# Four-layer graph network: edge sums begun by a flag instead of a zero product, and denominators cut at column 320

## The chip, the core and the metric

The kernel runs on one core of a Trainium2 chip. A core has a matrix engine (TensorE, in profiles PE, its weight loads PEld), a vector engine (VectorE, DVE), an activation engine (ScalarE, ACT), a general engine (GpSimd, POOL) and an engine that here only issues transfers (SyncE, SP). Products land in PSUM[...]. The metric is the time of the whole program on the device, in microseconds; lower is better.

## What is computed

There are 2708 nodes with 256 features, `x`, and one dense 2708 x 2708 matrix `adj` that is mostly zero. Four layers follow each other, each as `x = layernorm(x + layer(x))`. Layers 1 and 2, cut to what matters here:

```python
# layer 1: attention with 4 heads of 64 columns, all over the same mask
h = (x @ W).reshape(n, heads, head_dim)
e = src[:, :, None] + dst.T[None, :, :]
e = jnp.where(e > 0, e, ALPHA * e)
e = jnp.where(adj[:, None, :] > 0, e, NEG_INF)
out = jnp.einsum('nhm,mhd->nhd', jax.nn.softmax(e, axis=-1), h)
# layer 2, its first sum: the "edge sums"
node_support = node_adj_norm @ h        # adj without its diagonal, times x
edge_output = _gru_cell(node_support, h, edge_Wih, edge_Whh, edge_bih, edge_bhh)
```

The softmax of layer 1 needs for every node and head a sum of weighted features (the numerator, 64 values) and a sum of the weights alone (the denominator). Layer 2 then goes on with three attention heads over the same matrix, a second gated cell and layer 3's product.

## The kernel before, in words

The nodes are cut into 22 tiles of 128, the last with 20 rows. `adj` comes transposed, so that a block has source nodes on partitions and destination nodes along its columns. All products are float32; each float32 product leaves two records of a matmul in the profile.

**Layer 1.** Destinations are taken in six spans of tiles (4, 4, 4, 4, 3, 3), two at a time, so there are three groups: 1024, 1024 and 660 columns, the last made of spans of 384 and 276. For each group the heads are taken in two pairs (`q` = 0, 1), and for each pair the 22 source tiles `c` in turn. For each `c` VectorE makes two weight tiles `p`, one per head (L835). `heads` (L814, its product L817) multiplies 64 features of each head with `p` and sums into `acc[s]`, one bank for each span `s`, with the two heads in the two halves of the partitions. `totals` (its product L826) does the same with 32 columns of `h`, whose last is the one that gives the denominator; the four products of one `c`, two spans by two heads, go to the four 32-partition quarters of one bank, `den`. Quarter `j = 2 * (s ^ q) + i` belongs to span `s` and head `i`. The order is totals, heads for even `c` and heads, totals for odd `c`, so blocks of 16 records of one kind follow each other. At the end of a pair ScalarE copies both `acc` (L848) and then the two halves of `den` (L852) to SBUF. `step` weaves in the rows of the group before, in small steps: `layer1_end` (L683) transposes sums and denominators, divides, adds and normalises twice, with steps on ScalarE, VectorE (L679, L705, L708, L727, L730) and GpSimd (L680); `layer1_logits` (L748) transposes the finished rows on TensorE (L756) and multiplies them (L773). After the last group that group's own `layer1_end` runs beside the first edge sums.

**Layer 2's edge sums.** `raw_sums` (L354) works on six ranges `r` of 226 columns (the last 224) in each half of the destinations. For each of 11 pairs of source tiles it loads a block `pa` on SP's queue (five buffers), clears the diagonal on GpSimd (L286), and calls `seven` (L309), which forms three sums and a difference on VectorE (L315 to L318) and multiplies seven times (L328): a block product of two by two with seven products instead of eight. The seven results live in four banks: `m1` alone, and `m26`, `m75`, `m43` with two of them each, side by side. A product with `start=True` begins a sum; one without adds to what is there. Since two sums share a bank, before each range a product of a tile of zeros with a zero column (L359) is written over the whole of each shared bank with `start=True`, and the products in the shared banks carry no start flag (`not (one_bank and i)`). At the end of a range `gathered` (L332) reads the banks: ScalarE copies `m1` (L336), and VectorE adds the others to it in four steps (L339, L342, L345, L346). The result goes through a gated cell (L1062) for the first four ranges, with the sums one range ahead of the cells.

The order of instructions on each engine is drawn up by a scheduler from the program; the engines execute in that order and wait for each other by semaphores. Pools give out buffers in turn, and a new tile waits for the last reader of its buffer.

Of the kernel before, what the change touches and what calls it, by code (L numbers as in the profile page):

```python
# [10 lines left out]
BF16 = mybir.dt.bfloat16  # L11
# [8 lines left out]
P = 128  # L20
# [7 lines left out]
def kernel(  # L28
# [24 lines left out]
    nc = tc.nc  # L53
# [8 lines left out]
    W = GT * P  # L62
    CT = 32
# [28 lines left out]
    def width(lo, hi):  # L92
        return min(hi * P, N) - lo * P
# [19 lines left out]
    const = ctx.enter_context(tc.tile_pool(name="const", bufs=1))  # L113
# [5 lines left out]
    make_identity(nc, ident)  # L119
    offdiag = const.tile([P, P], F32, name="offdiag")  # L120
    nc.vector.tensor_scalar(offdiag, ident, -1.0, 1.0, ALU.mult, ALU.add)
    zeros = const.tile([P, P], BF16, name="zeros")
    nc.gpsimd.memset(zeros, 0.0)
    neg_half = const.tile([P, 1], F32, name="neg_half")
    nc.gpsimd.memset(neg_half, -0.5)

# [182 lines left out]
    def seven(pool, m, pa, b, tt, c, w, start, stop, slots, one_bank=False):  # L309

        m1, m26, m75, m43 = m
        a11, a21, a12, a22 = [pa[:, j, i, :w] for j in range(2) for i in range(2)]
        s = pool.tile([P, 3, pa.shape[3]], F32, tag="s", name="s", bufs=2)
        s1, s2, s4 = (s[:, i, :w] for i in range(3))
        nc.vector.tensor_tensor(s1, a21, a22, ALU.add)  # L315
        nc.vector.tensor_tensor(a21, a21, a11, ALU.subtract)  # L316
        nc.vector.tensor_tensor(s2, s1, a11, ALU.subtract)
        nc.vector.tensor_tensor(s4, a12, s2, ALU.subtract)  # L318
        for i, (dst, lt, rt) in enumerate((
            (m1, b[2 * c][:, :P], a11),  # L320
            (m26[:, 0], b[2 * c + 1][:, :P], a12),
            (m75[:, 0], tt[:, 2], a21),
            (m75[:, 1], tt[:, 0], s1),
            (m26[:, 1], tt[:, 1], s2),
            (m43[:, 0], tt[:, 3], a22),
            (m43[:, 1], b[2 * c + 1][:, P:], s4),
        )):
            nc.tensor.matmul(dst[:, :w], lt, rt, start=start and not (one_bank and i), stop=stop and not (one_bank and i in (1, 2, 5)))  # L328
            if i in slots:
                between()  # L330

# [22 lines left out]
    def raw_sums(pool, ps, keep, r):  # L354

        a, w = raws[r]
        m = [ps.tile([P, 2, W // 2], F32, tag=nm, name=nm) for nm in ("m1", "m26", "m75", "m43")]
        for b in m[1:]:
            nc.tensor.matmul(  # L359
                b.rearrange("p i w -> p (i w)"), zeros, zeros[:, :1].to_broadcast([P, W]), start=True, stop=False  # L360
            )
        m[0] = m[0][:, 0]
        for c in range(MH):
            pa = pool.tile([P, 2, 2, w], F32, tag="pa", name="pa", bufs=5)
            load_pairs(raws, r, c, pa)
            clear_own(raws, r, c, pa)
            if r == 0:
                xq.append(quarter_sums(keep, xs, c, "xq"))
            seven(pool, m, pa, xs, xq[c], c, w, c == 0, c == MH - 1, (), True)
            if c == MH - 1:  # L370
                y, _ = gathered(pool, m, w, w, "supt", 2)
                y = y.rearrange("p f h w -> p f (h w)")
                if r in left:
                    nc.scalar.dma_start(sup_d[r], y)
                edges.append(y)
            yield
# [27 lines left out]
    if True:  # L404
# [12 lines left out]
        if True:  # L417
# [38 lines left out]
            with pool("l0", 2) as l0:  # L456
# [48 lines left out]
                with pool("prep", side="right") as prep:  # L505
# [100 lines left out]
                    s = load_strip(l0, t)  # L606
# [21 lines left out]
                for t in range(ahead + 2, NT - 1):  # L628
                    s = load_strip(l0, t)
# [8 lines left out]
                s = load_strip(l0, t)  # L638
# [22 lines left out]
            if True:  # L661
# [123 lines left out]
                dens = [keepr.tile([P, W], F32, name=f"den{s}") for s in range(2)]  # L785
                for g in range(0, len(spans), 2):
                    segs = spans[g : g + 2]
                    at, w = segs[0][0] * P, width(segs[0][0], segs[-1][1])
                    if g >= 4:
                        falls.append(fallp.tile([P, H, 2 * W], F32, tag="fall_b", name="fall_b"))  # L790
                        for i in range(len(segs)):
                            load_fall(falls[-1], g + i, nc.sync)
                    cols = [(lo * P - at, width(lo, hi)) for lo, hi in segs]
                    sums, steps, halves = [], [itertools.chain(*rest)] if g == 0 else [], []

                    def step(c):
                        for s in list(steps):
                            if next(s, s) is s:
                                steps.remove(s)

                        if q == 0 and c % 5 == 1 and len(halves) < len(ended):
                            halves.append(layer1_end(l1, ended[len(halves)]))
                            next(halves[-1])
                            steps.append(itertools.islice(halves[-1], 2))

                        if q == 1 and c % 5 == 0 and c // 5 < len(halves):
                            steps.append(itertools.chain(halves[c // 5], [None], layer1_logits(ended[c // 5])))
                            next(steps[-1])

                    for q in range(H // 2):  # L810
                        den = ps_acc.tile([P, W], F32, tag="acc", name="den")
                        acc = [ps_acc.tile([P, W], F32, tag="acc", name="acc") for _ in segs]

                        def heads(c, ps, flags):  # L814
                            for s, (p0, ws) in enumerate(cols):
                                for i in (1, 0):
                                    nc.tensor.matmul(  # L817
                                        acc[s][i * HD : (i + 1) * HD, :ws], hs[c][:, 2 * q + i, :HD],
                                        ps[i][:, p0 : p0 + ws], **flags,
                                    )  # L820

                        def totals(c, ps, flags):
                            for s, (p0, ws) in enumerate(cols):
                                for i in (1, 0):
                                    j = (2 * (s ^ q) + i) * CT
                                    nc.tensor.matmul(  # L826
                                        den[j : j + CT, :ws], hs[c][:, 2 * q + i, HD + 1 - CT :],
                                        ps[i][:, p0 : p0 + ws], **flags,
                                    )

                        for c in range(NT):
                            ps = []
                            for i in range(2):
                                p = l1.tile([P, 2 * W], F32, tag="p", name="p", bufs=5)
                                nc.vector.scalar_tensor_tensor(  # L835
                                    p[:, :w], falls[g // 2][:, 2 * q + i, :w], rise[:, c, 2 * q + i : 2 * q + i + 1],
                                    mask[:, c, at : at + w], ALU.max, ALU.mult,
                                )
                                ps.append(p)

                            for part in (heads, totals)[:: -1 if c % 2 == 0 else 1]:
                                part(c, ps, dict(start=(c == 0), stop=(c == NT - 1)))
                                if part is (totals, heads)[c % 2]:
                                    step(c)
                        got = []
                        for s, (p0, ws) in enumerate(cols):
                            sb = keepr.tile([P, W], F32, tag=f"sum{q}{s}", name=f"sum{q}{s}")
                            nc.scalar.copy(sb[:, :ws], acc[s][:, :ws])  # L848
                            got.append(sb)
                        for s, (p0, ws) in enumerate(cols):  # L850
                            two = slice(2 * (s ^ q) * CT, 2 * ((s ^ q) + 1) * CT)
                            nc.scalar.copy(dens[s][two, :ws], den[two, :ws])  # L852
                        sums.append(got)
                    for a in steps:
                        for _ in a:
                            pass
                    ended = [(t, s, sums, dens, t - segs[0][0]) for s, (lo, hi) in enumerate(segs) for t in range(lo, hi)]
                    ended = [ended[i : i + 2] for i in range(0, len(ended), 2)]
# [24 lines left out]
                for i in range(SPLITS):  # L883
                    part = u_parts[:, :, i * K : (i + 1) * K]
# [7 lines left out]
                for t in range(NT):  # L892
                    for b, acc in zip(banks, pus):
                        w = width(*spans[b[0]])
                        for j, g in enumerate(b):
# [3 lines left out]
                                start=(t == 0), stop=(t == NT - 1),  # L899
# [801 lines left out]
```

## Time and profile before

| | us |
|---|---|
| median of 3 runs | 1865.03 (1864.9 to 1866.25) |
| the profiled execution | 1865.35 |
| its span, first to last instruction | 1863.6 |
| TensorE busy in it | 1832.7 |
| VectorE busy in it | 1280.9 |
| ScalarE busy in it | 699.3 |

The profile is of one execution. Its span leaves out what lies before the first and after the last instruction. A group's line gives engine, operation, output and inputs, shapes, how many there were, busy time, mean duration of one in ns, and the idle time of the engine before them with what ended it. A timeline's line gives start, length, engine and instructions that follow each other, with the idle time before. Ends of matmuls are modelled and hold their drain, so the distance from one start to the next is what a product costs in a stream; a few matmul records are missing.

### The profile page before, as it was taken

The numbers are of one execution on the slowest core, as the hardware profiler recorded it, in microseconds if no ns is written. First come the engines' busy times: TensorE is split into PE (matmuls) and PEld (weight loads), VectorE is DVE, ScalarE is ACT, GpSimd is POOL, SyncE is SP. The second block draws the span as 40 slices with busy tenths as digits, with TensorE's granted clock in tenths as the row PEclk, the third lists the DMA queues.
The fourth block names the chain that finished last, engine by engine and source line by source line (L and its number), as shares of the span: only waits on it lengthen the run. The fifth ranks groups of instructions, "written<-read, shape, count | busy, mean of one in ns | idle before, by whom it ended". The sixth has DMA issues, their size and how long they took to land. (4 is left out here: it accounts for less than half of the span.)

```text
span 1863.6 us, 23088 instructions
## 1 busy us (share of the span) xinstructions
PE 1832.7 (98%) x7526; PEld 1035.4 (56%) x7530; DVE 1280.9 (69%) x2263; ACT 699.3 (38%) x1442; POOL 266.4 (14%) x427
## 2 busy tenths in 40 slices
PE   9999999999999999999999999999999999999997
PEld 7788832233345887887444444444445556654555
DVE  5344489999897664754568888776887768844664
ACT  3544410033144203111546655555665556321011
POOL 1211220001012411000002000111200302111111
PEclk9999999999999999999999999999999999999999
DMA  8344410100002667754647666454554545634764
GB/s 298 133 148 151 168 30 1 30 1 12 12 7 71 144 144 186 182 130 114 182 131 207 176 174 171 123 159 114 165 151 121 135 106 141 167 106 116 203 163 121
DMA packets 435101, 237.32 MB, mean 127 GB/s; under 512 B 184363, under 2 KB 422348, under 8 KB 432540
## 3 DMA queue, kind: packets, MB, share of 16 engines
q1 hardware_dynamic: 422414, 208.66, 41.4%
q0 software_dynamic: 8208, 22.59, 3.9%
q10 hardware_dynamic: 4350, 4.50, 0.7%
q8 instruction: 62, 1.02, 0.2%
q14 instruction: 67, 0.55, 0.1%
HBM read 223.00 MB, written 12.66 MB: 126 GB/s over the span
## 5 line engine op out<-in xcount | busy, mean ns | idle before, releaser
L835 DVE SCALAR_TENSOR_TENSOR p<-fall_b,rise,mask 128x1024 f32<-128x1024 f32 (+1 forms) x264 | 293.9, 1156 | 32.5 <-PE den L826 16.7
L1328 ACT ACTIVATE p<-st,e_neg 128x1024 f32<-128x1024 f32 (+1 forms) x198 | 197.3, 1040 | 193.9 <-PE m L328 190.1
L328 PE MATMUL m<-s,xq 128*128 128x512 f32 (+3 forms) x660 | 230.1, 467 | 0.0
L817 PE MATMUL acc<-p,h 128*64 128x512 f32 (+2 forms) x1056 | 214.5, 548 | 0.2 <-ACT sum L848 0.2
L328 PE MATMUL m<-p,xq 128*128 128x512 f32 (+1 forms) x396 | 183.0, 544 | 0.1
L215 PE MATMUL acc<-turn,strip 128*128 128x257 f32 x792 | 181.8, 379 | 0.0
L1331 ACT ACTIVATE p<-p 128x1024 f32<-128x1024 f32 (+1 forms) x198 | 178.8, 942 | 0.2
L315 DVE TENSOR_TENSOR s<-p 128x512 f32<-128x512 f32 (+3 forms) x132 | 81.5, 618 | 136.6 <-PE m L328 112.7
L328 PE MATMUL m<-p,x 128*128 128x512 f32 (+1 forms) x396 | 167.7, 542 | 0.3 <-DVE supt L345 0.3
L328 PEld LDWEIGHTS m<-s,xq 128*128 128x128 f32 x660 | 124.5, 190 | 76.3 <-issue 59.2
L1332 DVE TENSOR_TENSOR p<-p,blk 128x1024 f32<-128x1024 f32 (+1 forms) x132 | 142.8, 1101 | 33.6 <-ACT p L1331 23.1
L215 PEld LDWEIGHTS acc<-turn,strip 128*128 128x128 f32 x792 | 147.2, 190 | 20.3
L817 PEld LDWEIGHTS acc<-p,h 128*64 128x64 f32 x1056 | 69.8, 136 | 138.2 <-issue 128.6
L328 PE MATMUL m<-s,x 128*128 128x512 f32 (+3 forms) x330 | 127.2, 467 | 0.0
L826 PE MATMUL den<-p,h 128*32 128x512 f32 (+2 forms) x1056 | 117.8, 548 | 0.0
L328 PEld LDWEIGHTS m<-p,xq 128*128 128x128 f32 x396 | 74.6, 190 | 76.9 <-issue 61.3
L328 PEld LDWEIGHTS m<-p,x 128*128 128x128 f32 x396 | 74.8, 190 | 75.5 <-issue 61.1
L474 ACT ACTIVATE below<-strip 128x384 bf16<-128x384 f32 x132 | 78.4, 594 | 68.4 <-DMA strip<-in_adj_t_dram 65.0
L316 DVE TENSOR_TENSOR p<-p 128x512 f32<-128x512 f32 (+3 forms) x132 | 82.3, 624 | 2.3
L328 PEld LDWEIGHTS m<-s,x 128*128 128x128 f32 x330 | 62.0, 190 | 39.2 <-issue 34.6
L318 DVE TENSOR_TENSOR s<-p,s 128x512 f32<-128x512 f32 (+3 forms) x132 | 81.2, 615 | 1.9
L286 POOL TENSOR_TENSOR blk<-blk,offdiag 128x128 f32<-128x128 f32 (+3 forms) x50 | 28.2, 566 | 376.0 <-DMA blk<-in_adj_t_dram 359.2
(288 smaller groups left out, 2591.9 us busy)
## 6 DMA issues: line engine op xcount, KB each, us to landing
strip<-in_adj_t_dram SPq DMA_DIRECT2D x19, 1408.0 KB, 6.0
blk<-in_adj_t_dram SPq DMA_DIRECT2D x88, 256.0 KB, 3.4
blk<-in_adj_t_dram SPq DMA_DIRECT2D x88, 192.0 KB, 4.1
pa<-in_adj_t_dram SPq DMA_DIRECT2D x110, 128.0 KB, 2.8
turn<-in_adj_t_dram SPq DMA_DIRECT2D x44, 256.0 KB, 3.1
blk<-in_adj_t_dram SPq DMA_DIRECT2D x88, 128.0 KB, 2.7
p<-in_adj_t_dram SPq DMA_DIRECT2D x88, 128.0 KB, 2.7
turn<-in_adj_t_dram SPq DMA_DIRECT2D x44, 192.0 KB, 3.1
```

The source lines that it names most:

```text
L215: at = nc.tensor.matmul(acc, s[:, c, :n], rhs(c), start=(c == 0), stop=(c == NT - 1))
L315: nc.vector.tensor_tensor(s1, a21, a22, ALU.add)
L316: nc.vector.tensor_tensor(a21, a21, a11, ALU.subtract)
L318: nc.vector.tensor_tensor(s4, a12, s2, ALU.subtract)
L328: nc.tensor.matmul(dst[:, :w], lt, rt, start=start and not (one_bank and i), stop=stop and not (one_bank and i in (1, 2, 5)))
L474: nc.scalar.activation(below[:, : (hi - lo) * P], s[:, lo:hi].rearrange("p c n -> p (c n)"), AF.Relu, scale=-1.0, accum_out=negative[:, BE ...
L817: nc.tensor.matmul(acc[s][i * HD : (i + 1) * HD, :ws], hs[c][:, 2 * q + i, :HD], ps[i][:, p0 : p0 + ws], **flags,)
L826: nc.tensor.matmul(den[j : j + CT, :ws], hs[c][:, 2 * q + i, HD + 1 - CT :], ps[i][:, p0 : p0 + ws], **flags,)
L835: nc.vector.scalar_tensor_tensor(p[:, :w], falls[g // 2][:, 2 * q + i, :w], rise[:, c, 2 * q + i : 2 * q + i + 1], mask[:, c, at : at + w] ...
L1328: nc.scalar.activation(p[:, :, :w], st_k[:, :, :w], AF.Relu, scale=-1.0, bias=e_neg[:, at, k : k + 1])
L1331: nc.scalar.activation(p[:, :, :w], p[:, :, :w], AF.Exp, scale=-1.0)
L1332: nc.vector.tensor_tensor(p[:, :, :w], p[:, :, :w], blk[:, i, :, :w], ALU.mult)
```

## The change

Two separate edits. In layer 2 the tile of zeros and its 18 products (six ranges, three banks) go, and the first product of each bank carries the start flag: results 0, 1, 2 and 5 of the seven, and not the second ones in a bank, 3, 4 and 6. In layer 1 the columns of a group are cut for the denominators at `cut`, a multiple of 64 near the middle: 512 for 1024 columns as before, and 320 for 660, so that the four products have 320 and 340 columns instead of 384 and 276. The numerators keep their spans. Since the parts of `den` no longer match the spans, the copies at the end of a pair go part by part: in the last group columns 0 to 319 and 320 to 383 of the first span from different quarters, then the second span, three copies instead of two.

```diff
-    zeros = const.tile([P, P], BF16, name="zeros")
-    nc.gpsimd.memset(zeros, 0.0)
...
-            nc.tensor.matmul(dst[:, :w], lt, rt, start=start and not (one_bank and i), stop=stop and not (one_bank and i in (1, 2, 5)))
+            nc.tensor.matmul(dst[:, :w], lt, rt, start=start and not (one_bank and i in (3, 4, 6)), stop=stop and not (one_bank and i in (1, 2, 5)))
...
-        for b in m[1:]:
-            nc.tensor.matmul(
-                b.rearrange("p i w -> p (i w)"), zeros, zeros[:, :1].to_broadcast([P, W]), start=True, stop=False
-            )
...
+                    cut = min(cols[1][0], (w // 2 + P // 4) // (P // 2) * (P // 2))
+                    halves_at = [(0, cut), (cut, w - cut)]
...
                         def totals(c, ps, flags):
-                            for s, (p0, ws) in enumerate(cols):
+                            for s, (p0, ws) in enumerate(halves_at):
...
-                            nc.scalar.copy(dens[s][two, :ws], den[two, :ws])
+                            for i, (a, n) in enumerate(halves_at):
+                                lo, hi = max(p0, a), min(p0 + ws, a + n)
+                                if lo < hi:
+                                    part = slice(2 * (i ^ q) * CT, 2 * ((i ^ q) + 1) * CT)
+                                    nc.scalar.copy(dens[s][two, lo - p0 : hi - p0], den[part, lo - a : hi - a])
```

## The prediction

> **What bounds the kernel now.** I read the busy line of the page first, then the groups by shape for the two pieces of work that the change touches, then short stretches of TensorE's timeline around them, and last the waits and the busy time by stretch. From the page:
>
> ```profile
> span 1863.6 us, 23088 instructions
> PE 1832.7 (98%) x7526; PEld 1035.4 (56%) x7530; DVE 1280.9 (69%) x2263; ACT 699.3 (38%) x1442; POOL 266.4 (14%) x427
> PEclk9999999999999999999999999999999999999999
> ```
>
> TensorE is busy 98% of the span at full clock, so time comes off where TensorE's own stream gets shorter and nothing else is waiting beside it. The groups by shape (busy is the union, then the mean of one):
>
> ```profile
> L826 PE MATMUL den<-p,h 128*32 128x384 f32 x176 | 32.7, 492 | 0.0
> L826 PE MATMUL den<-p,h 128*32 128x276 f32 x176 | 25.1, 402 | 0.0
> L359 PE MATMUL m<-zeros 128*128 128x512 bf16 x14 | 5.3, 379 | 0.2
> ```
>
> The mean of one is not its price: four denominator products run side by side in four column groups, and a record also holds its drain. So I take starts in TensorE's timeline instead: two pairs of column tiles in the last group of layer 1, then a pair in an earlier group where both halves are 512 wide.
>
> ```profile
> 505.20 1.49 PE L826 MATMUL den<-p,h 128*32 128x384 f32 x16
> 506.62 2.44 PE L817 MATMUL acc<-p,h 128*64 128x384 f32 x16
> 508.99 1.48 PE L826 MATMUL den<-p,h 128*32 128x384 f32 x16
> ...
> 466.27 1.92 PE L826 MATMUL den<-p,h 128*32 128x512 f32 x16
> 468.12 3.65 PE L817 MATMUL acc<-p,h 128*64 128x512 f32 x16
> ```
>
> A block of 16 denominator records (each float32 product leaves two) takes 506.62 - 505.20 = 1.42 us although half of them are only 276 wide, and 468.12 - 466.27 = 1.85 us when all are 512 wide. The length follows the wider half: (1.85 - 1.42) / (4 passes x 128 columns) = 0.84 ns a column and pass. The zero products, where layer 2 starts its second and fourth range:
>
> ```profile
> 632.34 0.39 PE L359 MATMUL m<-zeros 128*128 128x512 bf16 x1
> 632.57 0.93 PE L328 MATMUL m<-pa,x 128*128 128x226 f32 x4
> 633.33 0.55 PE L328 MATMUL m<-s,xq 128*128 128x226 f32 x2
> 633.71 0.38 PE L359 MATMUL m<-zeros 128*128 128x512 bf16 x1
> 633.93 0.54 PE L328 MATMUL m<-pa,xq 128*128 128x226 f32 x2
> ...
> 757.55 0.81 PE L359 MATMUL m<-zeros 128*128 128x512 bf16 x2
> 758.21 0.92 PE L328 MATMUL m<-pa,x 128*128 128x226 f32 x4
> ```
>
> One zero product delays its successor by 633.93 - 633.71 = 0.22 us; three in a row by 758.21 - 757.55 = 0.66 us (its third record is missing; 14 of 18 are there, but all 18 weight loads). The busy time by stretch tells which of these hold the end:
>
> ```profile
> 500.00:542.00 42.00, 42.00 (x356) 19.07 (x354) 40.41 (x78) 21.11 (x115) 5.16 (x5) 1.00 0.00 1
> 542.00:591.00 49.00, 48.77 (x412) 23.94 (x405) 38.32 (x56) 12.16 (x38) 10.05 (x20) 1.00 0.08 23
> 591.00:614.00 23.00, 20.00 (x98) 16.16 (x98) 19.69 (x85) 18.74 (x101) 8.36 (x12) 1.00 0.73 173
> 632.00:860.00 228.00, 227.59 (x1160) 174.57 (x1164) 127.11 (x308) 40.92 (x64) 25.84 (x57) 1.00 0.61 146
> ```
>
> After the length come TensorE's busy time, its weight loads, VectorE, ScalarE and GpSimd. TensorE fills the two stretches of the last group and everything from 632 on. In the first stretch VectorE is nearly full too (40.41 of 42). From 591 to 614 TensorE idles 3 us behind the layer-norm chain of the last tiles.
>
> **What the Trainium skill says.** "PSUM — Partial Sum Buffer", section "The four PSUM rules": the flag of a first product clears the written-marks of the whole bank, and a later product without it overwrites where the mark is clear. So one flag per bank does what the zero product did; no run here shows it yet. "TensorEngine Tiling (Array Packing)", "Key Properties": a change of tiling mode drains the engine. The trace agrees: the 276-wide column groups are done early, yet the 64-wide sums start at 506.62, after the 384-wide ones.
>
> **The change, step by step.**
>
> *Denominators.* The last group is 660 columns wide. Its halves go from 384 and 276 to 320 and 340, so the wider one loses 44 columns. There are 22 column tiles x 2 head pairs x 2 passes = 88 rounds of four: 88 x 44 x 0.84 ns = 3.25 us less on TensorE. The other two groups keep 512 and 512.
>
> Does VectorE allow it? Each p tile costs it 0.82 us from start to start, so 1.63 us a column tile against TensorE's (1.42 + 2.37) / 2 = 1.90, which becomes 1.82. In the first head pair it also carries layer-norm steps of the tiles before (`L727`, `L730`, 0.48 us each). In the instruction order of the changed program 9 of the 16 big steps stand in that half, against 13 before: four, about 1.9 us, go to the second half, where VectorE has 49.00 - 38.32 = 10.7 us free. 1.9 exceeds the 1.6 us by which TensorE gets faster in that half, so I take the whole 3.25. If VectorE held the first half back all the same, half is lost: 1.6 to 3.25.
>
> These four steps are late next. They feed ScalarE's normalised rows, which TensorE transposes (`L756`) in its fixed order. For the last pair the rows are ready at 566.31 + 1.08 = 567.4 and transposed at 585.80: 18 us to spare, and the move costs two column tiles, 3.8 us. ScalarE's wait for the four transposes of this stretch shows the same slack (total, times, longest):
>
> ```profile
> ACT turn L758 <- PE tr L756: 24.0, 4, 8.0
> ```
>
> *Copies.* Denominator columns 320 to 383 now lie in the second half's partitions, so ScalarE makes three copies instead of two per head pair. "ScalarE: Activation LUTs", "What ACT_TABLE_LOAD costs", prices an activation with constant scale at 186 ns + 0.83 ns a column, less 93 ns overlap with the next: for 64 columns an estimate of 0.15 us; the trace's 276-wide copy of 0.38 us agrees with that scale. The copy of the first half also gets shorter by 64 columns (0.05). At the first head pair no one waits. At the last the transposes of `den` (start 591.19) wait for them, and the layer-norm chain after it: 0.1 to 0.3 us, I take 0.2. Between the head pairs, before 543.24, TensorE idled 0.23 us for a ScalarE copy of `sum`; ScalarE now has fewer layer-norm steps ahead of it, 0 to 0.2 gained, I take 0.1.
>
> *Zero products.* 18 go. The first three (from 591.58, 0.65 us) stand where TensorE waits for ScalarE anyway: nothing, with 0.65 as the other end. The other 15 stand in stretches that TensorE fills: 15 x 0.217 = 3.25 us. The first product of each bank inherits the wait that the zero product had, for VectorE to have read the range before; behind it all later products queue. At the fourth to sixth range 18 us of gate products lie between: no wait. At the second the last read ends at 634.04, and the bank's first product would stand near 634.6; at the third it ends at 690.84 for a product near 691.1. Margins are 0.3 to 0.6 us, so I charge nothing; at worst the six zeros of these two return as waits, 1.3 us.
>
> *What moves.* The scheduler draws single first products of the next column tile ahead; their blocks landed and were cleared by 631.85, before 633.9. SP's queue takes two transfers of `xt` for the fourth range later, behind loads of `pa`; the third piece of that tile stood there already, at 796.58, and its gates start at 835.87: 39 us of cover. Removing the memset of `zeros` on GpSimd costs nothing; it ran before the first input had landed.
>
> **Sum.** -3.25 - 3.25 + 0.2 - 0.1 = -6.4 us. The profiled execution took 1865.35 us, its span 1863.6 and 1.75 us around it; it becomes 1858.95. The median of the runs, 1865.03, lies 0.32 below that execution, so I forecast 1858.6.
>
> **Rivals.**
> - VectorE becomes the bound in the first head pair. For it: 40.41 of 42 us busy, and p tiles ready only 0.2 us ahead in places. Against: the four steps moved out. Half of the denominators' gain goes: 1860.2.
> - The zero products are replaced by the wait that they covered. For it: margins of a few tenths at the second and third range. Against: no margin is below zero. At worst all 15 return: 1861.9.
> - The halves don't set the pace, and equal total columns mean equal time. The starts above speak against it. 1861.9 as well.
> - Slower: the layer-norm steps pushed back hold the transposes of the last pair, and with them TensorE's whole queue. It decides once they are over 18 us late, and makes the kernel slower beyond 18 + 6.4 = 24 us; at 28 us late it would be 1868.8. The order shows 3.8.
>
> **How the numbers follow.** Forecast 0.74 (1857.2 to 1860.0), VectorE 0.09, zeros' waits 0.09, halves 0.05, slower 0.03. A change within 0.2% (3.7 us) can't be told from none; the boundary is 1861.3. Faster takes the forecast, VectorE's case and a third of the zeros' case, which has values between 1858.6 and 1861.9: 0.74 + 0.09 + 0.03 = 0.86; same 0.11; slower 0.03. The range goes from 1857.0 (the first three zeros count too, both small terms come at their best, and 0.6 for the spread of the runs, 1.35 before) to 1861.9.
>
> **What would show it.** The 16-record denominator block at 1.27 us instead of 1.42, with TensorE still without idle time from 500 to 591 and layer 1's last product near 587.2 instead of 590.6; no records of `zeros`; the fourth range's first product right behind the last gate, 0.66 us sooner. Against me: idle time of TensorE behind `p` on VectorE near 500 to 542, or behind `supt` at the second or third range. I would be wrong if a stage after 860, whose order is the same, lost a different time to its waits, 0.9 to 1.8 us each at `L1220` and in layer 3, than now.

## The result, and the profile after

The changed kernel takes 1859.19 us (median of 8 runs, 1858.13 to 1861.14). The kernel before took 1865.68 us beside it (8 runs, 1864.9 to 1867.76). The ratio is 0.9964, with a 95% interval of 0.9955 to 0.9972: 6.5 us less by the medians, 5.2 to 8.4 by the interval. The forecast was 1858.6. A second series of the same kernel gave 0.9961 [0.9949, 0.9973]. A ratio uses all runs, so a difference worked out from it is not exactly that of the two medians.

The profiled execution took 1858.13 us, its span 1856.3. From its page, the length and the line of busy times:

```profile
span 1856.3 us, 23052 instructions
PE 1826.3 (98%) x7512; PEld 1031.6 (56%) x7512; DVE 1279.9 (69%) x2263; ACT 700.2 (38%) x1444; POOL 272.3 (15%) x426
```

TensorE's busy time fell by 6.4 us (1832.7 to 1826.3) and its share stayed at 98%: the time came out of its own stream. There is no group `m<-zeros` any more. The groups by shape of the last group's denominators (busy, mean ns):

```profile
L822 PE MATMUL den<-p,h 128*32 128x340 f32 x176 | 29.6, 455 | 0.0
L822 PE MATMUL den<-p,h 128*32 128x320 f32 x176 | 28.2, 438 | 0.0
```

Their means are again no prices. The starts are, in TensorE's timeline of the changed kernel (start, length): first a denominator block of the last group, then the end of the gates ahead of the sixth range.

```profile
505.41 1.35 PE L822 MATMUL den<-p,h 128*32 128x320 f32 x16
506.69 2.44 PE L813 MATMUL acc<-p,h 128*64 128x384 f32 x16
...
847.78 1.68 PE L1062 MATMUL gate<-supt,wih 128*128 128x452 f32 x4
849.30 0.92 PE L326 MATMUL m<-pa,x 128*128 128x224 f32 x4
```

The block takes 506.69 - 505.41 = 1.28 us, where it took 1.42. The range's first product now starts 849.30 - 847.78 = 1.52 us after the last gate products. The same place in the kernel before:

```profile
852.55 1.68 PE L1062 MATMUL gate<-supt,wih 128*128 128x452 f32 x4
854.07 0.81 PE L359 MATMUL m<-zeros 128*128 128x512 bf16 x2
854.72 0.92 PE L328 MATMUL m<-pa,x 128*128 128x224 f32 x4
```

Three zero products (one record is missing) stood between, one for each shared bank; a bank here holds a tile of 128 x 512 float32 values. It was 854.72 - 852.55 = 2.17 us: now 0.65 less.

Busy time by stretch of the changed kernel (length; TensorE, its weight loads, VectorE, ScalarE, GpSimd):

```profile
500.00:542.00 42.00, 42.00 (x370) 18.54 (x367) 40.27 (x74) 21.86 (x116) 6.11 (x6) 1.00 0.01 2
542.00:588.00 46.00, 46.00 (x397) 22.17 (x395) 38.42 (x59) 12.09 (x37) 10.83 (x20) 1.00 0.08 24
```

TensorE fills both head pairs of the last group. VectorE carries nearly as much as before in the first (40.27 of 42 us), and TensorE does not wait for it.

Where the 7.2 us of span went, from the starts of the same instructions in both traces:

| stretch | change, us |
|---|---|
| layer 0 | +0.4 |
| last group of layer 1, first denominators to last | -3.05 |
| start of layer 2 to the first node product, of which 0.65 per range are zeros | -3.8 |
| node stage and layer 3 | -0.8 |

### The profile page after: what moved, and what is told of

Read it like the earlier page. It is cut to its first block, busy times and chain, and to the rows that moved or that the text cites. A ratio compares the mean times of both kernels' runs of the same rounds, so it can differ in the third digit from the quotient of the medians.

```text
span 1856.3 us, 23052 instructions
## 1 busy us (share of the span) xinstructions
PE 1826.3 (98%) x7512; PEld 1031.6 (56%) x7512; DVE 1279.9 (69%) x2263; ACT 700.2 (38%) x1444; POOL 272.3 (15%) x426
## 4 chain that ended last, share of the span: by engine, by line
PE 85%; DMA 5%; DVE 4%; SPq 3%; issue 1%; ACT 1%; POOL 1%; POOLq 0%; DVEq 0%; ACTq 0%
PE m L326 40%; PE acc L813 11%; PE acc L213 8%; PE bank L1187 7%; PE den L822 6%; PE bank L1163 3%; SPq L273 2%; PE bank L1230 2%; PE gate L1062 2%; DMA strip<-in_adj_t_dram 2%; DMA p<-in_adj_t_dram 1%; PE pm L423 1%; PE pq L983 1%; PE m L1428 1%; DMA blk<-in_adj_t_dram 1%
```

## The experiments

My theory: a round of four denominator products lasts as long as its widest, and each zero product behind the first three costs TensorE 0.217 us. The rivals: equal totals cost equal time; zeros only covered waits; VectorE holds the first head pair; late layer-norm rows hold TensorE. Each kernel was timed beside the kernel before; ratios are to it.

### The denominators alone

In the kernel before, with the zero products kept:

```diff
+cut = min(cols[1][0], (w // 2 + P // 4) // (P // 2) * (P // 2))
+halves_at = [(0, cut), (cut, w - cut)]
...
-for s, (p0, ws) in enumerate(cols):
+for s, (p0, ws) in enumerate(halves_at):
     for i in (1, 0):
         j = (2 * (s ^ q) + i) * CT
...
-nc.scalar.copy(dens[s][two, :ws], den[two, :ws])
+for i, (a, n) in enumerate(halves_at):
...
```

> The kernel before with the new halves of 320 and 340 rows (and the three copies) in the last group of layer 1; the zero products stay. My theory, that a round of four denominator products lasts as long as its widest: 88 rounds x 44 columns x 0.84 ns = 3.25 us off, 0.2 back for the third copy, so 3.0 to 3.3 us faster than before, all of it in the last group, with the 16-record block at 1.27 to 1.28 us. If equal totals meant equal time: 0 to 0.2 slower. If VectorE held the first head pair: 1.6 faster, with idle time of TensorE behind p. If removing the zeros tile is what made layer 0 0.4 us longer, layer 1 starts here where it starts before, at 247.06 after the first product's own shift.

Measured: 1862.27 us beside 1865.33, ratio 0.9982 [0.9974, 0.9991], or 3.4 us less (1.7 to 4.9). TensorE's timeline in this kernel:

```profile
508.07 1.35 PE L828 MATMUL den<-p,h 128*32 128x320 f32 x16
509.36 2.44 PE L819 MATMUL acc<-p,h 128*64 128x384 f32 x16
```

The block takes 1.29 us by these rounded starts. From the first denominators of the last group to the last, the trace is 3.05 us shorter than before, the same 3.05 as in the changed kernel, so in this stretch the flags change nothing. Equal totals do not mean equal time, and VectorE did not take half of it back.

The side question on layer 0 went neither way. Here, with the `zeros` tile in place, layer 1 starts at 250.14, 3.1 us later than before. TensorE's timeline shows why:

```profile
52.11 0.37 PE L444 MATMUL pf<-ident,fall 128*4 128x128 f32 x1 [3.30 <-DVE h L436]
```

And the busy time by stretch, whose last three figures are the granted clock, the DMA share and GB/s:

```profile
50.00:60.00 10.00, 7.89 (x34) 6.61 (x35) 1.98 (x7) 2.17 (x9) 2.23 (x4) 0.83 0.01 2
```

TensorE waited 3.30 us for `h` (0.7 before), and the granted clock of these 10 us was 0.83 on average. Two other programs of this study (the worse cut and more work on VectorE) show 0.83 in the same stretch and start layer 1 about 2 us late. Layer 0 differs by up to 3.1 us between single executions, and single profiles must be compared stage by stage.

### The flags alone

In the changed kernel:

```diff
-cut = min(cols[1][0], (w // 2 + P // 4) // (P // 2) * (P // 2))
+cut = cols[1][0]
```

> The changed kernel with the old halves of 384 and 276 rows: the flags alone. My theory: the first three zero products were hidden, the other 15 cost 0.217 us each, so 3.25 us faster than before. If the trace of the changed kernel is right that the order of work in the ranges also shifts, 3.3 to 3.9. If waits took the place of the zeros: 0 to 2 faster, with idle time of TensorE in front of the first products of the ranges. If all 18 counted: 3.9. No zeros tile here: if its removal is what shifts layer 0, layer 1 starts 0.4 us later than before.

Measured: 1860.06 us beside 1865.33, ratio 0.9975 [0.9965, 0.9984], 4.7 us less (3.0 to 6.5). Its last group lasts exactly as long as before. From there to the first node product its trace is 4.9 us shorter. Of these, 1.0 and 0.4 us are stalls in the profile of before, behind the products at 881.88 and 718.19, that other runs of kernels with zero products do not have; what remains is about 3.5. The runs reject a return of the zeros as waits (0 to 2 us less); they can't tell 15 counted zeros from 18 (3.9). By the medians the two parts alone save 3.1 and 5.3 us, together 8.3, and the whole change 6.5 and, in its second series, 7.5. Each of these is uncertain by about 2 us, so that the parts add up rests on the traces.

### The zero products doubled

In the kernel before:

```diff
-for b in m[1:]:
+for b, first in [(b, f) for b in m[1:] for f in (True, False)]:
     nc.tensor.matmul(
-        b.rearrange("p i w -> p (i w)"), zeros, zeros[:, :1].to_broadcast([P, W]), start=True, stop=False
+        b.rearrange("p i w -> p (i w)"), zeros, zeros[:, :1].to_broadcast([P, W]), start=first, stop=False
     )
```

> The kernel before with every zero product issued twice (36 instead of 18), the second adding zeros to the bank. My theory: each of the 15 later ones costs its 0.217 us, so 3.25 us slower than before, 0.65 us at each of the second to sixth range; the six at the start of the first range still hide behind the layer-norm chain. If zero products only cover waits that would be there without them: 0 to 1.5 slower. If the first range's count too: 3.9.

Measured: 1868.58 us beside 1865.46, ratio 1.0016 [1.0008, 1.0024], 3.0 us more (1.5 to 4.5). TensorE's timeline ahead of the sixth range:

```profile
856.72 1.68 PE L1062 MATMUL gate<-supt,wih 128*128 128x452 f32 x4
858.24 1.47 PE L359 MATMUL m<-zeros 128*128 128x512 bf16 x6
859.54 0.92 PE L328 MATMUL m<-pa,x 128*128 128x224 f32 x4
```

Six zero products take 859.54 - 858.24 = 1.30 us, 0.217 each. (They are bf16 and leave one record each; not all products are float32.) They start right at the place of the first product, with no wait before them. They are work, not cover for a wait.

### The first three zero products put back

In the changed kernel, with the old flags for range 0:

```diff
+for b in m[1:] if r == 0 else ():
+    nc.tensor.matmul(
+        b.rearrange("p i w -> p (i w)"), zeros, zeros[:, :1].to_broadcast([P, W]), start=True, stop=False
+    )
```

> The changed kernel with the zero products of the first range alone put back (three, 0.65 us). Read by its trace: the time from the last denominator product of layer 1 to the last edge product ahead of the layer's row transposes is 23.0 to 23.25 us in the two profiles of the changed kernel. My theory, that they hide behind the layer-norm chain: within 0.25 of that. If they count: 23.65 or more.

The stretch from the start of the last denominators to the start of the row transposes takes 30.82 us in its one profile: 0.06 more than in one profile of the changed kernel (30.76), 0.31 more than in the other (30.51). The times named in the expectation are some 7 us too small for this stretch; the steps between its cases stand. This alone leaves it between the two cases. Two other kernels speak for hidden zeros: with six of them there (the doubled ones) the stretch takes 30.84 us, with none (the flags alone) 30.64. The wait decides. TensorE's timeline where layer 1 ends, in this kernel:

```profile
587.23 0.78 PE L828 MATMUL den<-p,h 128*32 128x320 f32 x8
...
588.91 0.81 PE L360 MATMUL m<-zeros 128*128 128x512 bf16 x2
...
590.46 0.44 PE L694 MATMUL tr<-ident,sum 128*128 128x128 f32 x2 [0.30 <-ACT turn L712]
```

And the changed kernel itself:

```profile
587.12 0.78 PE L822 MATMUL den<-p,h 128*32 128x320 f32 x8
...
590.35 0.44 PE L688 MATMUL tr<-ident,sum 128*128 128x128 f32 x2 [0.94 <-ACT turn L706]
```

From the start of the last denominators to these transposes both take 3.23 us. With the three zeros TensorE waits 0.30 us for ScalarE; without them, 0.94. Their 0.65 us came off the work and went onto the wait.

### A worse cut

```diff
-cut = min(cols[1][0], (w // 2 + P // 4) // (P // 2) * (P // 2))
+cut = min(cols[1][0], 256) if w < 2 * W else cols[1][0]
```

> The changed kernel with the last group's denominators halved at 256: 256 and 404 rows, the same total of 660. My theory (the widest of a round sets it): 404 - 340 = 64 columns more, 88 x 64 x 0.84 ns = 4.73 us slower than the changed kernel, so about 1.7 us faster than before; the 16-record block at 1.49 us. If equal totals mean equal time: as the changed kernel, 6.5 us faster than before.

Measured: 1863.01 us beside 1865.33, ratio 0.9988 [0.9982, 0.9995], 2.2 us less than before (0.9 to 3.4), and so, by the ratios, 4 to 5 us more than the changed kernel. TensorE's timeline:

```profile
503.46 1.56 PE L822 MATMUL den<-p,h 128*32 128x256 f32 x16
504.96 2.44 PE L813 MATMUL acc<-p,h 128*64 128x384 f32 x16
```

The block takes 1.50 us for the same 660 columns that take 1.28 when cut at 320. The last group is 5.3 us longer than in the changed kernel. Two waits of TensorE for ScalarE's `turn`, 0.18 and 0.64 us, cover the 0.6 above the 4.73 expected.

### An even cut

```diff
-cut = min(cols[1][0], (w // 2 + P // 4) // (P // 2) * (P // 2))
+cut = min(cols[1][0], w // 2)
```

> The changed kernel with equal halves of 330 and 330 rows instead of 320 and 340. My theory: the wider half sets it, so 88 rounds x 10 columns x 0.84 ns = 0.74 us faster than the changed kernel, 7.4 faster than before, with the 16-record block at 1.24 us. If VectorE has no more to give in the first head pair: the same as the changed kernel, with TensorE idle behind p.

Measured: 1858.26 us beside 1865.46, ratio 0.9963 [0.995, 0.9976], no different from the changed kernel. The denominator blocks did shrink, to 1.25 us. TensorE's timeline in the first head pair shows where the gain went:

```profile
514.66 2.59 PE L813 MATMUL acc<-p,h 128*64 128x384 f32 x16
...
518.43 2.56 PE L813 MATMUL acc<-p,h 128*64 128x384 f32 x16
```

Sum blocks that last 2.44 us otherwise last 2.59 and 2.56, and a third 2.47; in the middle of each of the three, TensorE's weight load waits for VectorE's `p`. The first head pair is only 0.03 us shorter than in the changed kernel, the second 0.33. The first rival of the prediction begins here: in this order of work, VectorE's `p` tiles give the first pair no more than the 44 columns that the change took.

### Far fewer denominator columns

```diff
 for s, (p0, ws) in enumerate(halves_at):
+    if g == 4 and 2 < c < NT - 1:
+        ws = P
```

> The changed kernel with part of the denominators left out: in the last group column tiles 3 to 20 sum only the first 128 rows of each half. How near is VectorE's limit? If TensorE alone set the pace of both head pairs: 18 tiles x 4 rounds x 212 columns x 0.84 ns = 12.8 us faster than the changed kernel, 19.3 faster than before. My theory: VectorE is busy 40.3 of 42 us in the first head pair, so that pair can give about 1.7 us, while the second (38.4 of 46 busy) gives its whole 6.4: 8.1 us faster than the changed kernel, 14.6 faster than before, with TensorE idle behind p in the first pair alone.

Measured: 1857.18 us beside 1865.33, ratio 0.9958 [0.9946, 0.997], 7.8 us less than before. Both expectations fell: of 12.8 us of work taken from TensorE, the time shows about one against the changed kernel, no more than the intervals allow for noise. The waits of TensorE from 497 to 590 (total, times, longest):

```profile
PE tr L750 <- ACT x L738: 3.5, 3, 2.0
PE den L824 <- DVE p L833: 1.0, 2, 0.8
PE acc L813 <- DVE p L833: 0.2, 1, 0.2
```

The first line is the prediction's slow rival at work: TensorE reaches its transposes of the layer-norm rows before the rows are there, and everything queues behind them. The trace adds up so, against the changed kernel: 12.8 us of columns gone; 6.3 back as waits and stretched blocks behind `x` and `p`; about 1.5 at half clock (shown below); about 3.8 because the scheduler, with the new lengths, splits the stream into 27 more blocks of one kind, at 0.14 us each (a sum block of 16 records takes 2.37 us, two of 8 take 2.52); the last group ends up 0.4 us shorter, and 0.8 is not accounted for. My mistake was to treat the two head pairs as independent budgets. Work put off from the first pair comes due in the second as rows that TensorE waits for.

### More work on VectorE

```diff
 ps.append(p)
+if g == 4 and q == 0:
+    spare = l1.tile([P, P], F32, tag="spare", name="spare", bufs=1)
+    nc.vector.tensor_scalar(spare, ps[1][:, :P], 0.5, None, ALU.mult)
```

> The changed kernel with one more VectorE instruction of 128 columns in each of the 22 column tiles of the last group's first head pair, whose result no one reads; about 0.2 us each, 4.4 us in all. If VectorE's spare time in that pair (1.7 us) is all there is: 2.7 us slower than the changed kernel, 4.0 faster than before, with TensorE idle behind p. If the layer-norm steps simply move on into the second pair, as their order in this program does: no more than 1 us slower than the changed kernel.

Measured: 1857.85 us beside 1865.46, ratio 0.9958 [0.9946, 0.9971]. The 22 extra instructions took 4.8 us of VectorE, and the last group became only 0.16 us longer than in the changed kernel. The scheduler moved layer-norm steps on: two of `L721` and one of `L724` are left between 497 and 544, where the changed kernel has five and four. So the 1.7 us of spare time were no bound: what the first pair can take depends on how many steps the order leaves in it. In the even cut's order 10 columns were too many; in this one 4.8 us more found room.

### The changed kernel again

> The changed kernel once more, for a second profile of it. If the stalls that its first profile shows in the third range (0.42 us at 758.67 and 0.64 us at 775.24, TensorE behind blocks that VectorE and GpSimd prepare) and the 0.7 us longer layer 0 belong to the change, they stand here again at the same products. If they are the scatter of single executions, as the other runs of the same order suggest, they are gone or stand elsewhere, by up to 1 us each and 3 us in layer 0. Time 6.0 to 6.9 us under before.

Measured: 1857.98 us beside 1865.46, ratio 0.9961 [0.9949, 0.9973]. By the medians that is 7.5 us less, more than the 6.0 to 6.9 expected, and within the interval (5.0 to 9.5). The stalls (they stand in the fourth range; the expectation counts from zero) are gone in this profile: from the gates ahead of it to the gates after it, the range is 1.34 us shorter than in the first profile. Layer 1 starts at 247.11, against 247.06 before and 247.49 in the first profile. Neither belongs to the change. But from the first node product to the end this profile takes 963.8 us and the first 961.0: near 1613 TensorE waits 2.10 us for a transfer, and then runs at half clock for 3.4 us.

### A try at a better kernel: quarter sums first

In the first range TensorE waits for blocks that VectorE prepares. While layer 1 ends, VectorE sits idle for 4.2 us. So its quarter sums `xq` for the first five (or eight) column tiles were asked for ahead of the last layer-norm steps, with the even cut.

```diff
+for c in range(5):
+    xq.append(quarter_sums(xqp, xs, c, "xq"))
 ahead = itertools.chain.from_iterable(raw_sums(eblk, ps_s, xqp, r) for r in range(len(raws)))
...
-if r == 0:
+if r == 0 and len(xq) <= c:
     xq.append(quarter_sums(keep, xs, c, "xq"))
```

> The kernel with halves of 330 rows, and the quarter sums (xq) of the first five column tiles of layer 2 asked for before the layer-norm steps of the last pairs, so that VectorE does them in the 4.2 us in which it waits for the end of layer 1, and not between the later blocks of the first range. My theory: TensorE's waits for VectorE in the first range (0.5 + 0.3 + 0.7 + 0.6 + 1.4 us in the kernel with halves of 330) go in part: 1 to 3 us faster than that kernel, 8 to 10 faster than before. If the layer-norm chain or the landing of pa blocks holds the range: no difference to it, 7.2 faster than before.

> The same with eight column tiles: 6.6 us of VectorE work for 4.2 us of waiting, so the first reciprocals of the layer-norm chain start some 2 us later. If that chain has the slack that I see (its rows are not waited for in the first profile): as with five tiles or up to 1 us faster. If it has not: 1 to 2 us slower than with five tiles.

Measured, beside 1867.51 us before: 1859.14, ratio 0.9955 [0.9939, 0.9971], and 1858.92, ratio 0.9951 [0.9936, 0.9965]. The intervals hold the changed kernel's 0.9961 and 0.9964, and the traces show no gain: from the start of layer 1's last denominators to layer 2's first logit sums (`pu`) it takes 45.50 and 45.58 us, against 45.55 with the even cut alone. TensorE's waits from 586 to 618, with five tiles:

```profile
PE m L326 <- DVE pa L314: 1.2, 4, 0.4
...
PE m L326 <- POOL o_rs L674: 0.7, 1, 0.7
```

With the even cut alone:

```profile
PE m L326 <- DVE pa L314: 2.3, 4, 1.2
```

The wait for VectorE halved. It came back as waits for transfers of `pa` (2.1 us with five tiles) and for GpSimd, which clears a block behind layer-norm steps of its own. The edge products up to that last wait come 0.8 us sooner than with the even cut alone, and the row transposes start at the same time. With eight tiles no wait for VectorE is left, and those for `pa` are 2.9 us. No version here beats the changed kernel by a measurable amount.

## Why the prediction was right

The forecast from 1865.03 was -6.4 us; the medians differ by 6.5. Step by step:

| step of the sum | forecast, us | the runs showed |
|---|---|---|
| denominators | -3.25 | -2.9: the block went from 1.415 to 1.281 us, 0.134 x 22 |
| wait before 543.24 | -0.1 | about -0.2: the wait is gone |
| first three zeros | 0 | 0: the wait behind them grew from 0.30 to 0.94 us |
| other 15 zeros | -3.25 | -3.0 (1.5 to 4.5) by doubling, about -3.5 by the trace without them |
| third copy | +0.2 | not seen: the transposes that wait for ScalarE start 3.23 us after the last denominators with three copies, 3.38 with two |

*The price of a column.* I took 0.84 ns from the 384 and 512 wide blocks. Blocks of 330, 340 and 404 columns (1.248, 1.281, 1.494 us) give 0.83 ns, and put 512 at 1.855 where 1.85 was measured. The 384 and 276 block of before lies 13 ns below their line, so it had a little less to lose: 2.9 instead of 3.25.

*The third copy.* It lasts 0.20 us in the trace and holds the next copy for 0.23, where the prediction's estimate was 0.15. But the first copy, which the chain needs first, now ends 1.25 us after the start of the last denominators instead of 1.40, and that is what counted. The smaller gain on the denominators and the copy that cost nothing largely cancel in the sum.

*The first range.* The three zeros did hide behind a wait for ScalarE. But the prediction put all 3 us of idle time from 591 to 614 down to the layer-norm chain; by the trace 2.4 us of it are waits for blocks `pa` that VectorE prepares, and 0.3 the wait for ScalarE.

*The waits at the second and third range.* I charged nothing on margins of 0.3 to 0.6 us, and kept 1.3 us as the other end. The kernel with flags alone has no wait there; the one with eight quarter sums first waits 0.19 us at the third range, so the margin is thin. In the Trainium skill, "PSUM — Partial Sum Buffer", section "The four PSUM rules", said that one flag per bank is enough; the changed kernel begins all its edge sums that way, and they come out right.

*VectorE in the first head pair.* I argued that four moved steps (1.9 us) exceed the 1.6 us that TensorE gains. The conclusion held, but by less than it seemed: 10 columns more, and `p` came late. The chance of 0.09 was for a neighbour very near.

*The slow rival.* I priced it from the last pair's 18 us of slack. With much shorter denominators it appeared at earlier pairs, with rows late by 2.0 and 0.8 us. One pair's slack in one order was no bound for the others. (Two side figures of the prediction don't add up exactly: 28 us late gives 1868.6, not 1868.8, and the lower end of the range 1857.15, not 1857.0.)

The last stages, which I held to be unchanged, differ by 2.8 us between the two profiles of the changed kernel, and the trace's 7.2 us hold 0.4 more in layer 0 and 0.8 less in the last stages that the sum did not have. The close hit is therefore partly luck: the interval of the ratio is 3.2 us wide.

## What to carry to other kernels

Where column groups run side by side, cut the work so that the groups are equally wide; the widest was paid for here, at 0.83 ns a column and pass. An instruction that only prepares a bank costs its full length (here 0.217 us) on the engine that is full, and nothing where that engine waits next anyway: look for the wait behind it before you count it. A cut on the bounding engine stays a gain only until the next engine's order of work is met, here within 10 columns more; try one step more before you trust the slope.

## What I had not expected of the hardware

TensorE's granted clock halved in the middle of the program, after waits of two or three microseconds. In the kernel with eight quarter sums first, TensorE waited 1.50 and 1.38 us with a few products in between; busy time by stretch after that (the third figure from the end is the granted clock):

```profile
594.00:596.00 2.00, 2.00 (x7) 1.77 (x7) 1.72 (x8) 2.00 (x14) 0.00 (x0) 0.50 0.75 168
```

And in the kernel with fewer denominator columns, after the wait of 1.98 us for `x`:

```profile
558.00:560.00 2.00, 2.00 (x10) 0.63 (x8) 1.04 (x2) 0.40 (x1) 0.00 (x0) 0.50 0.00 0
```

In the first case the records of products of 226 columns came every 377 ns instead of every 190 from 594 to 599. In the Trainium skill, "TensorE: Matmul & The Clock Gate", section "What's actually happening", describes a clock of half rate after an idle window of about 3.4 us. The trace agrees on the half rate, but no unbroken idle time of 3.4 us came before it: single waits of 1.98, 2.10, 2.12 and 2.21 us were enough in four profiles, or twice 1.4 to 1.5. Nor does the length of the wait alone decide: with five quarter sums first, a wait of 2.44 us near 1611 left the clock at 1.00, and in layer 0 waits for `h` of up to 1.9 us did. What else decides, the runs here do not show.

All 13 profiles have a stretch at half rate at the end of the program, and six have one earlier. By the clock records this earlier one lasts 3.41 us in five of them, from 557.59 to 561.00 in the second case above, and 6.82, twice that, in the first. In layer 0 the waits for `h` of 2.1, 2.2 and 3.3 us each went with one, and these three profiles are the ones that start layer 1 two to three microseconds late. So a wait on an engine that is 98% busy can cost more than its length: at half rate, up to 1.7 us more in 3.41.
